# Cross attention on one core: four chunks' queries by seven products instead of eight, and the order written anew

## The chip, the cores and the metric

The kernel runs on one core of a Trainium2 chip. The metric is device time in microseconds (us), the median of three runs. All data are float32. The engines are TensorE (PE in the profile; its weight loads are PEld), VectorE (DVE), ScalarE (ACT), GpSimd (POOL) and SyncE (SP), which issues nearly all DMAs.

## What is computed

Two batches of 2048 tokens of 640 channels attend, with 20 heads of 32 channels, to a context of 154 tokens of 1024 channels. The first 77 context tokens (text) and the last 77 (image) have their own key and value weights and their own softmax; the two results are added.

```python
q = split_heads(x @ Wq.T)
k, v = split_heads(text @ Wk.T), split_heads(text @ Wv.T)
k_ip, v_ip = split_heads(ip @ Wk_ip.T), split_heads(ip @ Wv_ip.T)
out = merge(attend(q, k, v)) + merge(attend(q, k_ip, v_ip))   # softmax(q k / sqrt(32)) v
return out @ Wo.T + bo + x
```

The launch lays every matrix out with the contracted dimension first, so x is xT (640 x 4096), and the output is written as outT.

## The kernel before

Channels are cut into five chunks of 128 (four heads each), tokens into blocks of 512, four blocks in a batch. A *step* u is one chunk of one batch for two blocks (1024 tokens): twenty steps, q = u // 2 counts batch and chunk (0 to 4 are batch 0, 5 to 9 batch 1). A step's tokens are handled in three *groups* s: groups 0 and 1 of three tiles of 128 tokens ("large", 3 x 4 heads x 2 softmaxes of 77 = 1848 columns), group 2 of two tiles ("small", 1232 columns).

What is done for a step and group, each a word in a list:

- `q.u.h` (`queries`, L196, matmuls L201): the queries of one chunk for block h of step u, five matmuls of 512 columns over the five slices k of the contraction; `cq` scales them by ScalarE into a tile of `qpool` (L211).
- `Rs.u` (`scores`, L226): scores into four PSUM banks, one half of the eight (`@0` or `@1`).
- `Ks.u` (`take`, L245): ScalarE copies the four banks to SBUF (`pb`).
- `Ms.u` (`maxima`): VectorE's maximum of each row, from SBUF (L281), or, for the groups in `DIRECT`, from PSUM by four reductions (L284) with no K.
- `Ss.u` (`subtract`, L295): GpSimd subtracts the maxima. Groups in `DIRECT` and `BIASED` have no S: their exponential takes the maximum as its bias, row by row (L269), and those also in `SUMMED` get the row sums from it (no D).
- `Es.u` (exponential, L301 or L269, ScalarE), `Ds.u` (`sums`, L306, VectorE's denominators), `Is.u` (`invert`, L311, VectorE), `Ns.u` (`normalise`, L316, GpSimd), `Ts.u` (`transpose`, L323, VectorE).
- `A.q` (`attend`, L332): attention of both steps of a chunk; it waits for their six T. `CA` copies it out by ScalarE (L355, L359).

Around these stand the projections of keys and values (`k`, `v`, L142, with `ck`, `cv`), the output projection of batch 0 by seven products for eight (`m`, L490 and the fifth matmuls L500, taken by VectorE in `cm`, L515 and L521; GpSimd makes their token sums `G`, L431, and weight sums `W`, L401; `o` is the last chunk, L471), and, after A.9, the output projection of batch 1 by 33 products (`F`, L848) whose sums of weights and of rows (`V`, L828; `X`, L834) VectorE and GpSimd make, and whose results VectorE adds (`Y`, L792 and L794) and SP stores (L798).

The order is not derived at run time: `SCHEDULE` (L562) is a list of words, a planner's output, and `emit` issues them one after the other. Each engine executes its own words in the list's order, and waits only where data or a buffer demand it. SP's words are in the list too (`LK`, `LQ`, `LX` loads, `VS` spreads of values, `SF` and `SS` for batch 0's output), and one that waits holds the ones behind it.

Ahead of the list stands the opening (L524 to L559): loads of the first block by slices alternating with 64 KB slices of Wq on SP and ACT, the next loads, seven dummy matmuls (L549), queries of blocks 0 and 1 for chunk 0 and of block 0 for chunk 1, and the first two key projections.

Of the kernel before, what the change touches and what calls it, by code (L numbers as in the profile page):

```python
# [20 lines left out]
def kernel(  # L21
# [43 lines left out]
        (11, 0), (13, 0), (13, 2), (14, 0), (14, 2), (15, 1), (15, 2), (16, 2), (18, 1),  # L65
    }
    BIASED = {
        (2, 2), (3, 2), (4, 2), (5, 2), (6, 2), (7, 2), (9, 2), (11, 2), (12, 0), (12, 2), (18, 2), (19, 0),
        (19, 2),
    }  # L70
    SUMMED = {
        (4, 2), (6, 2), (11, 2), (12, 0), (12, 2), (13, 0), (13, 2), (14, 0), (15, 1), (15, 2), (18, 1),
        (18, 2), (19, 2),
# [7 lines left out]
    qpool = ctx.enter_context(tc.tile_pool(name="qpool", bufs=5))  # L81
    small = ctx.enter_context(tc.tile_pool(name="small", bufs=4))
    psum = ctx.enter_context(tc.tile_pool(name="psum", bufs=1, space=bass.MemoryType.PSUM))
# [3 lines left out]
    wqs = [const.tile([P, NC, P], F32, name=f"wq_{n}") for n in range(3)]  # L87
    bo_sb = const.tile([P, NC], F32, name="bo_sb")
    kT = const.tile([P, NC, B, 2, L], F32, name="kT")
# [77 lines left out]
    slices = []  # L167

    def load_x(queue=nc.sync):

        if slices:
            i, k = slices.pop(0)
            queue.dma_start(out=xs[i][:, k], in_=xT[ts(k, P), ts(i, TB)])

    XROOM = NHB - 1

    def place_of(u, h):
        _, b, _, sub = step_of(u)  # L180
        return late.index((u, h)) % XROOM if b else sub * NH + h

    def load_block(u, h):

        tokens = ds(S + (step_of(u)[3] * NH + h) * TB, TB)
        nc.sync.dma_start(
            out=xs[place_of(u, h)], in_=xT[:, tokens].rearrange("(k p) t -> p k t", p=P)
        )

    def load_wq(q):  # L190
        c = q % NC
        nc.sync.dma_start(
            out=wqs[q % 3], in_=WqT[:, ts(c, P)].rearrange("(k p) o -> p k o", p=P)
        )
# [3 lines left out]
    def queries(u, h, pq):  # L198
        q = step_of(u)[0]
        for k in range(NC):  # L200
# [7 lines left out]

    def take_queries(u, h, pq):
        qT = qpool.tile([P, TB], F32, tag="qT", name=f"qT_{u}_{h}")  # L210
        nc.scalar.mul(qT, pq, SCALE)  # L211
        qTs[(u, h)] = qT
# [13 lines left out]
    def scores(u, s, ps):  # L226
# [3 lines left out]
        for t in range(n):  # L230
            h, st = divmod(first + t, TB // P)
            for g in range(G):
# [6 lines left out]
                )  # L239

# [73 lines left out]
    def normalise(u, s):  # L314
        n = GROUPS[s][1] * G
        nc.gpsimd.tensor_tensor(  # L316
            rows_of(u, s), rows_of(u, s), rdens[(u, s)].unsqueeze(3).to_broadcast([P, n, 2, L]), ALU.mult
        )
# [205 lines left out]
    slices.extend((i, k) for i in range(NHB) for k in range(NC))  # L524
    queues = nc.sync, nc.scalar
    for k in range(NC):
        load_x(queues[k % 2])
        queues[1 - k % 2].dma_start(out=wqs[0][:, k, :], in_=WqT[ts(k, P), :P])
    for _ in range(NC):
        load_x()  # L530
    load_wq(1)
    half = NCC // 2
    for k in (0, half):
        nc.sync.dma_start(  # L534
            out=wo_ct[:, ds(k * B * LT, half * B * LT)].rearrange("p (k n) -> p k n", k=half),
            in_=ctxT[ds(k * P, half * P), :].rearrange("(k p) n -> p k n", p=P),
        )
        load_w(k // half)
    for _ in range(NH * NC):
        load_x()  # L540
    load_w(2)
    load_w(3)
    load_wq(2)
    nc.sync.dma_start(out=bo_sb, in_=bo.rearrange("(c p) -> p c", p=P))

    warm = pb[:, 0, 0].rearrange("p g l -> p (g l)")[:, :P]
    nc.vector.memset(warm, 0.0)
    for _ in range(7):
        nc.tensor.matmul(banks[0][:, :P], warm, warm, start=True, stop=True)  # L549
    FIRST = ((0, 0), (0, 1), (2, 0))  # L550
    for n, (u, h) in enumerate(FIRST):
        queries(u, h, banks[G + n])
        take_queries(u, h, banks[G + n])
    for t in range(2):

# [335 lines left out]
```

## Time and profile before

| | us |
|---|---|
| median of three runs | 497.44 |
| lowest and highest run | 497.38, 497.64 |
| span of the profiled execution | 496.7 |
| TensorE's first scores, start | 24.4 |
| attention of chunk 5, start | 254.7 |
| last matmul's add, start | 493.0 |

The span is the time from the first to the last instruction of the profiled execution, which is the only time the profile gives for it; the runs' median lies 0.7 us above. In the profile L12 is line 12 of the kernel. A row of a group of instructions reads: line, engine, operation, what it writes <- what it reads, shapes, count | busy us, mean ns of one | idle time of the engine before them, and what ended it. In the chain of waits the columns are start, length and what ran. In the table by stretches each engine's busy us stands before the number of its instructions in brackets.

### The profile page before, as it was taken

To read this page: it belongs to the slowest core of one execution; us is meant where nothing else is said; L and a number is where in the kernel's file an instruction comes from. 1 tells how busy PE (TensorE), PEld (TensorE's weight loads), DVE (VectorE), ACT (ScalarE), POOL (GpSimd) and SP (SyncE) were. 2 spreads that over 40 slices of the span, in tenths; PEclk is the share of its full clock that TensorE was granted. 3 is DMA by queue.
4 is the path that set the end of the run, shared out by engine and by line. 5 is a ranking of instruction groups with operands and counts; after the bars stand their busy time and mean duration, and the time that the engine had idled before them with its cause. 6 is when DMAs were issued, how large, how long until landed. Compare 5 with 4: busy or idle time off the path is not lost.

```text
span 496.7 us, 10482 instructions
## 1 busy us (share of the span) xinstructions
PE 490.3 (99%) x4114; PEld 287.9 (58%) x4114; DVE 408.5 (82%) x412; ACT 315.0 (63%) x1021; POOL 362.5 (73%) x157
## 2 busy tenths in 40 slices
PE   8999999999999999999999999999999999999997
PEld 5676657657547556456647654755755675444442
DVE  0069989979979989969976896687999978898877
ACT  1165878978978778668999786587578966100000
POOL 0069978798888999989874858565899888284830
PEclk9999999999999999999999999999999999999999
DMA  8991440332360454886445177418525401420115
GB/s 259 356 246 40 132 120 1 106 93 69 92 213 3 132 178 132 274 273 237 158 152 191 58 244 210 133 57 246 174 69 171 127 23 43 149 84 1 43 73 223
DMA packets 67474, 69.38 MB, mean 140 GB/s; under 512 B 5473, under 2 KB 47201, under 8 KB 67425
## 3 DMA queue, kind: packets, MB, share of 16 engines
q1 hardware_dynamic: 66704, 68.00, 43.8%
q8 instruction: 32, 0.52, 0.5%
q10 hardware_dynamic: 720, 0.72, 0.4%
q14 instruction: 18, 0.14, 0.1%
HBM read 54.94 MB, written 10.49 MB: 132 GB/s over the span
## 4 chain that ended last, share of the span: by engine, by line
PE 92%; DMA 3%; SPq 1%; DVE 1%; POOL 1%; ACT 1%; issue 0%; POOLq 0%
PE bank L201 33%; PE bank L848 11%; PE bank L490 10%; PE bank L233 10%; PE bank L332 10%; PE bank L142 9%; PE bank L471 6%; PE bank L500 3%; DMA aT<-in_L_xattn_Wk_ip_dram 2%; DMA wq<-in_L_xattn_Wq_dram 2%; SPq L534 1%; POOL pb L316 1%; DVE den L306 0%; ACT pb L301 0%; SPq L132 0%
## 5 line engine op out<-in xcount | busy, mean ns | idle before, releaser
L316 POOL TENSOR_TENSOR pb<-pb,rden 128x1848 f32<-128x1848 f32 (+1 forms) x60 | 176.1, 2944 | 39.7 <-DVE rden L311 35.5
L201 PE MATMUL bank<-x,wq 128*128 128x512 f32 x400 | 180.4, 601 | 0.6 <-DMA x<-in_x_dram 0.5
L295 POOL TENSOR_TENSOR pb<-pb,mx 128x1848 f32<-128x1848 f32 (+1 forms) x38 | 119.3, 3152 | 51.8 <-DVE mx L281 51.5
L201 PEld LDWEIGHTS bank<-x,wq 128*128 128x128 f32 x400 | 74.1, 191 | 86.7 <-issue 80.8
L323 DVE STREAM_TRANSPOSE pb<-pb 128x1920 f32<-128x1920 f32 (+1 forms) x60 | 115.7, 1932 | 4.9 <-POOL pb L316 4.3
L281 DVE TENSOR_REDUCE mx<-pb 128x24 f32<-128x1848 f32 (+1 forms) x51 | 93.7, 1850 | 30.7 <-ACT pb L245 30.5
L245 ACT COPY pb<-bank 128x462 f32<-128x462 f32 (+1 forms) x204 | 87.2, 539 | 36.0 <-PE bank L233 35.4
L306 DVE TENSOR_REDUCE den<-pb 128x24 f32<-128x1848 f32 (+1 forms) x47 | 88.7, 1895 | 17.6 <-ACT pb L301 13.3
L301 ACT ACTIVATE pb<-pb 128x1848 f32<-128x1848 f32 (+1 forms) x38 | 64.2, 1696 | 17.8 <-POOL pb L295 17.5
L269 ACT ACTIVATE pb<-pb,mx 128x77 f32<-128x77 f32 x224 | 67.8, 364 | 0.3 <-DVE mx L281 0.2
L233 PEld LDWEIGHTS bank<-kT,qT 32*128 32x128 f32 x1280 | 45.4, 184 | 26.9 <-issue 15.6
L269 ACT ACTIVATE pb<-bank,mx 128x77 f32<-128x77 f32 x184 | 51.8, 386 | 9.3 <-DVE mx L284 9.3
L233 PE MATMUL bank<-kT,qT 32*128 32x154 f32 x1280 | 56.2, 305 | 0.3 <-ACT kT L559 0.3
L332 PE MATMUL bank<-pb,v 32*32 32x512 f32 x1600 | 55.2, 597 | 0.0
L142 PE MATMUL bank<-wo_ct,aT 128*128 128x154 f32 x320 | 45.6, 296 | 0.3 <-DMA aT<-in_L_xattn_Wk_ip_dram 0.3
L142 PEld LDWEIGHTS bank<-wo_ct,aT 128*128 128x128 f32 x320 | 42.9, 188 | 3.6 <-issue 2.2
L332 PEld LDWEIGHTS bank<-pb,v 32*32 32x32 f32 x1600 | 29.9, 103 | 22.8 <-issue 10.7
L211 ACT ACTIVATE qT<-bank 128x512 f32<-128x512 f32 x40 | 24.2, 619 | 22.1 <-PE bank L201 22.0
L471 PE MATMUL bank<-aT,wo_ct 128*128 128x512 f32 x80 | 36.1, 596 | 0.0
L269 ACT ACTIVATION_READ_ACCUMULATOR pb<-bank,mx 128x1 f32 x128 | 33.6, 267 | 0.0
L490 PE MATMUL bank<-aT,wo_ct 128*128 128x256 f32 x128 | 32.3, 385 | 0.0
L490 PEld LDWEIGHTS bank<-aT,wo_ct 128*128 128x128 f32 x128 | 23.7, 190 | 6.5 <-issue 3.0
(75 smaller groups left out, 434.4 us busy)
## 6 DMA issues: line engine op xcount, KB each, us to landing
x<-in_x_dram SPq DMA_DIRECT2D x20, 1280.0 KB, 6.7
out_dram<-acc SPq DMA_DIRECT2D x20, 256.0 KB, 2.3
x<-in_x_dram SPq DMA_DIRECT2D x18, 256.0 KB, 5.9
acc<-in_x_dram SPq DMA_DIRECT2D x16, 256.0 KB, 4.7
out_dram<-x SPq DMA_DIRECT2D x15, 256.0 KB, 2.0
v<-vS SPq DMA_DIRECT2D x160, 20.0 KB, 2.8
wq<-in_L_xattn_Wq_dram SPq DMA_DIRECT2D x9, 320.0 KB, 5.0
aT<-in_L_xattn_Wk_dram SPq DMA_DIRECT2D x5, 512.0 KB, 5.5
```

The costliest lines, as they stand in the source:

```text
L142: nc.tensor.matmul(keys_in(out), loaded[n][:, k, :], cT[:, k, :, t, :], start=(k == 0), stop=(k == NCC - 1))
L201: nc.tensor.matmul(pq, wqs[q % 3][:, k, :], xs[place_of(u, h)][:, k, :], start=(k == 0), stop=(k == NC - 1),)
L233: nc.tensor.matmul(ps[g][:, ts(t, 2 * L)], qTs[(u, h)][g * D : (g + 1) * D, ts(st, P)], kT[g * D : (g + 1) * D, c, b].rearrange("p t l -> ...
L245: nc.scalar.copy(keys_of(u, s)[:, :, g], ps[g][:, : n * 2 * L].rearrange("p (n l) -> p n l", n=n))
L269: nc.scalar.activation(row, row if ps is None else rows_in(ps[g], n)[:, t, x], AF.Exp, bias=maxs[(u, s)][:, *one], accum_out=None if den i ...
L281: nc.vector.tensor_reduce(mx, rows_of(u, s), AX.X, ALU.max, negate=negate)
L295: nc.gpsimd.tensor_tensor(rows_of(u, s), rows_of(u, s), maxs[(u, s)].unsqueeze(3).to_broadcast([P, n, 2, L]), ALU.subtract)
L306: nc.vector.tensor_reduce(den_of(u, s), rows_of(u, s), AX.X, ALU.add)
L316: nc.gpsimd.tensor_tensor(rows_of(u, s), rows_of(u, s), rdens[(u, s)].unsqueeze(3).to_broadcast([P, n, 2, L]), ALU.mult)
L323: nc.vector.transpose(p, p)
L332: nc.tensor.matmul(pa[r][g * D : (g + 1) * D, :], v4s[q % 2][rows, g, k, :], zones[rows, :, g, k, :], start=(k == 0), stop=(k == NK - 1),)
L490: nc.tensor.matmul(part, w_of[m][:, kp, op], t_of(m, b, i)[:, kp], start=(op == kp == 0 and m in (1, 2, 5)), stop=(op == 1 and kp == 1 and ...
```

## The change

- **Queries of batch 1, chunks 0 to 3.** Chunks are taken in pairs (0, 1) and (2, 3). For a pair and a block, the four contraction slices form a 2 x 2 grid of two slices each, the block's tokens are halved (256 each), and the two chunks are the two outputs: a product of 2 x 2 blocks, made by seven products of sums instead of eight (`n`, `pair_product`, `take_pair`). The fifth slice is added into four of the products. Sums of tokens (`t`, four per block, GpSimd) and of weights (`WS`, GpSimd) are made once; the token sums of a block, 1 MB, are stored in DRAM (`TO`) and fetched again (`TI`) for the second pair. A product's result goes into PSUM; ScalarE writes four of the seven (`cn1`, `cn6`, `cn7`, `cn4`) to half a query tile, VectorE adds the other three.
- The query tiles so made early, for steps 12, 13, 16 and 17, are parked in DRAM (`QO`) and fetched again (`QI`). Chunk 4 of batch 1 and all of batch 0 keep the five matmuls.
- Blocks of batch 1 are loaded by `BX` (once for each pair) and, for chunk 4, `LX`.
- **Normalisations.** The nine groups in `SCALED` are normalised by VectorE.
- `DIRECT`, `BIASED`, `SUMMED` hold other groups.
- **Opening.** The first loads are words of the list (`XS`, `WA`, `LC`), fewer and larger, Wq's first two chunks together in rows of 1 KB; block 0 is multiplied by chunks 0 and 1 slice by slice (`qs`). Nine dummy matmuls.
- **End.** The last product `F32.0` and its add go by halves of 256 columns.
- **The list** is written anew; it holds 1172 words, before 1024.

What the two lists hold (the opening counted in; "to T" is up to the last transpose that chunk 5 needs):

| words | before | after |
|---|---|---|
| queries / products `n` / output products `m` in all | 40 / 0 / 28 | 24 / 56 / 28 |
| the same ahead of `A.5` | 29 / 0 / 4 | 20 / 37 / 6 |
| changes from scores or attention to other matmuls, in all (ahead of `A.5`) | 50 (27) | 51 (29) |
| groups in `DIRECT` / `BIASED` / `SUMMED` / `SCALED` | 9 / 13 / 13 / 0 | 17 / 10 / 13 / 9 |
| subtractions large / small, in all | 33 / 5 | 24 / 9 |
| normalisations on VectorE large / small, in all | 0 / 0 | 4 / 5 |
| to T: maxima from SBUF large / small | 24 / 13 | 19 / 9 |
| to T: maxima from PSUM large / small | 1 / 0 | 7 / 4 |
| to T: denominators large / small | 24 / 9 | 21 / 12 |
| to T: normalisations on VectorE large / small | 0 / 0 | 3 / 4 |
| to T: VectorE's products `cn`, `cm` | 0, 2 | 13, 3 |
| loads of a whole block | 20 | 12 |

The diff, cut to its core:

```diff
@@
     DIRECT = {
-        (11, 0), (13, 0), (13, 2), (14, 0), (14, 2), (15, 1), (15, 2), (16, 2), (18, 1),
+        (1, 1), (1, 2), (2, 0), (2, 2), (3, 1), (4, 1), (6, 1), (7, 1), (8, 1), (9, 2), (11, 2), (13, 0),
+        (13, 2), (15, 2), (16, 0), (19, 0), (19, 2),
     }
...
+    SCALED = {
+        (2, 2), (4, 0), (6, 2), (7, 2), (8, 0), (10, 0), (10, 2), (12, 1), (16, 2),
+    }
@@
+    FAR = [u for u in range(NC * SUB, NU - SUB) if (u // SUB - NC) % 2]
...
+    def put_away(u, h):
+        in_far[(u, h)] = far.tile([P, TB], F32, tag=f"qd_{u}_{h}", name=f"qd_{u}_{h}")
+        nc.sync.dma_start(out=in_far[(u, h)], in_=qTs.pop((u, h)))
+        q_free.append(q_place[(u, h)])
...
+    def sum_tokens(m, i, eng):
+        x, y = {
+            5: (tokens_in(i, 0, 0), tokens_in(i, 0, 1)),
+            7: (tokens_in(i, 0, 1), tokens_in(i, 1, 1)),
+            6: (sum_of(5, i), tokens_in(i, 1, 1)),
+            4: (sum_of(6, i), tokens_in(i, 1, 0)),
+        }[m]
+        eng.tensor_tensor(sum_of(m, i), x, y, ALU.add)
...
+    def pair_product(m, i, pair, ps):
+        w, last = weights_of(pair)
+        raw = {1: (0, 0), 2: (1, 0), 3: (1, 1)}
+        x = tokens_in(i, *raw[m]) if m in raw else sum_of(m, i)
+        fifth = {2: 0, 4: 0, 5: 1, 3: 1}.get(m)
+        for k in range(2):
+            nc.tensor.matmul(
+                ps[:, :HT],
+                w[m][:, k],
+                x[:, k],
+                start=(k == 0 and m in (1, 2, 5)),
+                stop=(k == 1 and fifth is None),
+                skip_group_check=True,
+            )
+        if fifth is not None:
+            nc.tensor.matmul(
+                ps[:, :HT],
+                last[m],
+                xs[i % 2][:, NC - 1, ts(fifth, HT)],
...
+    def take_pair(m, i, pair, ps):
+        u, h = 2 * (NC + 2 * pair) + i // NH, i % NH
+        if m in (7, 4, 5):
+            u += SUB
...
+        out = qTs[(u, h)][:, ts(int(m in (6, 3, 7, 5)), HT)]
+        if m in (1, 6, 7, 4):
+            nc.scalar.mul(out, ps[:, :HT], SCALE if m in (1, 4) else -SCALE)
+        else:
+            nc.vector.scalar_tensor_tensor(out, ps[:, :HT], SCALE, out, ALU.mult, ALU.add)
@@
-        nc.gpsimd.tensor_tensor(
+        (nc.vector if (u, s) in SCALED else nc.gpsimd).tensor_tensor(
             rows_of(u, s), rows_of(u, s), rdens[(u, s)].unsqueeze(3).to_broadcast([P, n, 2, L]), ALU.mult
         )
@@
-    for _ in range(7):
+    for _ in range(9):
         nc.tensor.matmul(banks[0][:, :P], warm, warm, start=True, stop=True)
...
+        "XS.0.0.1 WA.0.1 XS.0.1.1 WA.1.2 XS.0.3.1 XS.0.2.1 WA.3.2 XS.0.4.1 XS.1.2.3 XS.1.0.2 LC.0.4 LK.0 LC.4.4 LK.1 "
+        "LQ.2 qs.2.0.0.1@5 XS.2.0.2 XS.3.0.2 SF.0.3 XS.2.2.3 qs.0.0.0.1@3 qs.2.0.1.1 qs.0.0.1.1 qs.0.0.2.1 qs.0.0.3.1 "
+        "qs.0.0.4.1 XS.3.2.3 SF.0.2 SF.0.0 SF.0.1 SF.0.4 qs.2.0.2.1 qs.2.0.3.1 qs.2.0.4.1 cq.2.0 cq.0.0 LB "
+        "qs.0.1.0.1@2 qs.0.1.1.4 k.0.0@5 LK.4 cb.0.0.0 cb.0.0.1 k.0.1@0 cq.0.1 LK.3 LK.2 cb.0.1.0 cb.0.1.1 R2.0@1 "
+        "R0.0@0 K2.0 K0.0 M2.0 M0.0 S2.0 E2.0 LK.5 D2.0 S0.0 I2.0 N2.0 R1.0@1 K1.0 q.1.0@0 M1.0 E0.0 cq.1.0 S1.0 D0.0 "
...
+        "I1.7 E2.7 E0.7 D2.7 k.4.1@4 I2.7 q.8.1@7 D0.7 N2.7 T2.7 ck.4.1 k.4.0@0 ck.4.0 cq.8.1 BX.1 q.9.0@5 cq.9.0 "
+        "N1.7 R2.8@0 K2.8 M2.8 I0.7 t5.0.p WS.0.0 t6.0.p t7.0.p T1.7 R0.8@1 R1.8@0 t4.0.p K0.8 M0.8 N0.7 n1.0.0@4 "
+        "M1.8 T0.7 S0.8 v.4.1@7 TO.0 cn1.0.0 E2.8 D2.8 n6.0.0 cn6.0.0 E1.8 D1.8 E0.8 D0.8 I1.8 I2.8 q.9.1@5 n7.0.0 "
+        "cn7.0.0 n5.0.0@6 t5.1.p LQ.7 A.3@0 t7.1.p n4.0.0 I0.8 WS.0.1 CA.3 cv.4.1 cn5.0.0 t6.1.p N2.8 t4.1.p N0.8 "
...
+        "Y0.1.10 F32.0.0 F32.0.1 Y4.0.20.0 Y4.0.20.1 "
@@
+    def add_half(o, ps, op, half):
+        t, part = sum_at(o)[:, ts(half, HT)], ts(half, HT)
+        assert o not in untouched and parts_left[o] == 1
+        nc.vector.tensor_tensor(t, t, ps[:, part], op)
+        m, i = o
+        nc.sync.dma_start(out=outT[ts(m, P), ds(S + i * TB + half * HT, HT)], in_=t)
```

More of the change, by code (lines that the diff above doesn't have):

```diff
@@ L679, in emit @@
             queries(x, y, at[name])
+        elif k == "qs":
+            first, n = (int(a) for a in args[2:])
+            if where:
+                at[f"q.{x}.{y}"] = banks[int(where)]
+            queries(x, y, at[f"q.{x}.{y}"], range(first, first + n))
         elif k == "cq":
```

181 lines of the change are left out of this document (122 added, 59 removed), and 126 rows, old and new, of the table SCHEDULE.

## The prediction

> **What bounds the kernel now.** I read the page first, then the chain of waits in order of time, then who waits for whom, then busy time by stretches. The page names TensorE:
>
> ```profile
> span 496.7 us, 10482 instructions
> PE 490.3 (99%) x4114; PEld 287.9 (58%) x4114; DVE 408.5 (82%) x412; ACT 315.0 (63%) x1021; POOL 362.5 (73%) x157
> ```
>
> Busy matmuls need not be matmuls at their peak, so the chain has to say whether something else hides behind that 99%. Its columns are start, length, what; every TensorE matmul in float32 leaves two records, so "x10" is five matmuls.
>
> ```profile
> 13.68 8.00 DMA aT<-in_L_xattn_Wk_ip_dram
> ...
> 24.41 1.96 PE bank L233 x48
> 26.37 4.49 PE bank L201 x10
> ...
> 31.60 4.41 PE bank L142 x32
> 36.01 4.29 PE bank L201 x10
> ...
> 222.57 1.06 PE bank L490 x4
> 223.64 0.43 PE bank L500 x2
> 224.07 0.86 PE bank L490 x4
> ...
> 254.70 5.45 PE bank L332 x148
> ...
> 493.03 0.69 DVE acc L794
> ```
>
> Until 24.41 (the first scores) the chain waits for loads; from there to 493.03 it is matmul after matmul, and the end is one VectorE add and its store. The list of waits, asked for TensorE from 26 us to 496 us, has one entry in all:
>
> ```profile
> PE bank L490 <- DVE acc L515: 0.2, 1, 0.2
> ```
>
> So TensorE is the bound and its order runs without holes. An edit counts by what it does to TensorE's work, and by whether it opens a hole. The engine most likely to open one is VectorE, which makes the transposed probabilities that each attention word (L332) waits for:
>
> ```profile
> core 0: us, PE busy (x) PEld busy (x) DVE busy (x) ACT busy (x) POOL busy (x), PEclk, DMA share, GB/s
> 27.40:254.70 227.30, 227.13 (x2195) 137.99 (x2199) 209.34 (x163) 180.66 (x486) 198.22 (x71) 1.00 0.45 134
> 347.00:389.00 42.00, 42.00 (x392) 25.97 (x387) 39.86 (x38) 31.08 (x101) 38.34 (x16) 1.00 0.43 136
> ```
>
> From its first maximum (27.4) to the attention of chunk 5 (254.7) VectorE is idle for 227.3 - 209.3 = 18.0 us. That number is the whole question below.
>
> **The products (removed from TensorE).** A query word is five matmuls of 512 columns: 4.29 us in the row at 36.01. Four chunks by four blocks are sixteen such words, 68.6 us. In their place stand eight sets (two pairs of chunks by four blocks) of seven products. A product is two matmuls of 256 columns, and four of the seven carry a fifth: 18 matmuls, each 0.43 us by L490 (0.86 for two) and L500 (0.43 for one). That is 7.74 us a set, 61.9 us for eight: **6.8 us less** (6.7 to 6.9, with the rounding). Small matmuls could be held by their weight loads instead (the first row is the query line of today, for later):
>
> ```profile
> L201 PE MATMUL bank<-x,wq 128*128 128x512 f32 x400 | 180.4, 601 | 0.6 <-DMA x<-in_x_dram 0.5
> L490 PEld LDWEIGHTS bank<-aT,wo_ct 128*128 128x128 f32 x128 | 23.7, 190 | 6.5 <-issue 3.0 <-DVE acc L521 0.3 <-ACT pb L269 0.2
> ```
>
> A load takes 0.190 us and the matmul record beside it 0.215 (0.86 for four), so it fits, with little to spare; the new products have the shape of L490 and I price them by it. What is not hidden is the first load after scores or attention: 1.06 at 222.57, after scores, against 0.86 at 224.07, so 0.20. If each of the 56 products paid it the gain would be gone (11.2 us); but this falls due only where the kind of work changes. I count such changes in both lists: 50 and 51. I take +0.3 (0.2 for one more step out, about as much for the step in).
>
> **The opening.** The work before the first scores is the same: three queries and two key projections, 12.9 + 4.4 = 17.3 us (rows at 36.01 and 31.60), and so are the bytes ahead of the second key weights (two blocks, two chunks of Wq, the context, two key weights). What changes is the order: the first block is multiplied by two chunks as its slices land, so each slice gives twice the work, and the loads are fewer and larger. Nine dummy matmuls stand for seven:
>
> ```profile
> 1.05 3.35 PE L549 MATMUL bank<-pb 128*128 128x128 f32 x14 [1.05 <-DVE pb L547]
> ```
>
> They end at 1.05 + 9/7 x 3.35 = 5.4. If TensorE never starves after that, the scores begin at 5.4 + 17.3 + 0.3 (the copy of the keys) = 23.0; if the key weights land where they do now (13.68 + 8.00 = 21.7), at 24.4 again; and the second scores of the opening now need the half of PSUM that the first ones fill, so up to 0.5 of waiting for four copies is new. Bounds -1.4 and +0.5; I take **-0.4**.
>
> **The end.** The last matmul and its add go by halves, so that after the last matmul an add of 256 columns is left instead of 512: 0.69 becomes about 0.43 (L515 below); the store behind it stays. **-0.3** (0 to -0.5).
>
> **GpSimd.** Rows for both edits:
>
> ```profile
> L316 POOL TENSOR_TENSOR pb<-pb,rden 128x1848 f32<-128x1848 f32 x40 | 131.3, 3288 | 24.8 <-DVE rden L311 22.7 <-ACT aT L355 1.1 <-ACT pb L245 0.6
> L316 POOL TENSOR_TENSOR pb<-pb,rden 128x1232 f32<-128x1232 f32 x20 | 45.1, 2255 | 14.9 <-DVE rden L311 12.8 <-ACT kT L686 2.1
> L431 POOL TENSOR_TENSOR aT<-aT 128x512 f32<-128x512 f32 x8 | 10.2, 1278 | 0.1
> ```
>
> Four large and five small normalisations leave (24.4 us), nine large subtractions leave and four small ones come (about 20 us fewer at the price of L316); 16 token sums come at 1.28 (20.4) and eight weight sums of up to 256 columns (some 6). So 362 us becomes about 344: no bound by itself. But the sums stand close together, around chunks 3 to 5.
>
> **VectorE.** Rows for what changes ahead of chunk 5's attention:
>
> ```profile
> L281 DVE TENSOR_REDUCE mx<-pb 128x24 f32<-128x1848 f32 x35 | 71.5, 2051 | 28.4 <-ACT pb L245 28.3
> L281 DVE TENSOR_REDUCE mx<-pb 128x16 f32<-128x1232 f32 x16 | 22.6, 1409 | 2.3 <-ACT pb L245 2.2
> L284 DVE TENSOR_REDUCE mx<-bank 128x6 f32<-128x462 f32 x20 | 11.4, 631 | 5.7 <-ACT qT L211 3.0 <-PE bank L233 2.7
> L284 DVE TENSOR_REDUCE mx<-bank 128x4 f32<-128x308 f32 x16 | 6.5, 470 | 1.1 <-PE bank L233 1.1
> L515 DVE SCALAR_TENSOR_TENSOR acc<-bank,bo_sb,acc 128x256 f32<-128x256 f32 x32 | 13.7, 468 | 7.0 <-PE bank L500 7.0
> L834 DVE TENSOR_TENSOR pb<-aT 128x1024 f32<-128x1024 f32 x7 | 8.3, 1221 | 1.7 <-PE bank L332 1.5 <-ACT aT L359 0.2
> ```
>
> Up to the last transpose that chunk 5 needs (counts in the table of the change): five large maxima from SBUF fewer (-10.3), six more from PSUM at four reductions of 11.4/20 = 0.57 (+13.7); four small ones fewer (-5.6), four more from PSUM at 4 x 6.5/16 (+6.5); three large denominators fewer and three small ones more (same shapes as the maxima, -6.2 +4.2); 13 products taken at 13.7/32 = 0.43 (+5.6), one more output product (+0.9). Seven normalisations come. The trace shows none on VectorE: by a reduction of the same size one costs 2.05 and 1.41, by L834 scaled to its length 2.2 and 1.5. I take 2.1 and 1.4, so +11.9. Sum +20.7.
>
> In the same stretch TensorE gets more to do before chunk 5, because work moves ahead: 37 products (40.3) for nine queries (38.6), two output products (4.3), two more changes of kind (0.8): +6.8 less 0.4 of the opening. VectorE's first maximum comes about 1.2 earlier relative to the first scores (a small group is first). Idle time left: 18.0 + 6.4 + 1.2 - 20.7 = **4.9 us in 235**. It must work 98% of that stretch, where now it works 92%. After chunk 5 the room grows again, as fewer products are left.
>
> What made it idle so far:
>
> ```profile
> DVE mx L281 <- ACT pb L245: 29.4, 6, 26.4
> DVE den L306 <- ACT pb L301: 10.4, 10, 2.9
> ```
>
> (26.4 of the first row lies before the first maximum.) Most of the rest is denominators waiting for an exponential. An engine with more queued up waits less, and 17 groups instead of nine now go to ScalarE straight from PSUM without a subtraction, so I expect the 18 to shrink to 5 or 6, and give TensorE **+1.2** for what is left (0 to 4).
>
> [...] GpSimd and VectorE are seen to hold each other up, near the end:
>
> ```profile
> 421.10 0.46 POOL L828 TENSOR_TENSOR pb<-pb,wo_ct 128x128 f32<-128x128 f32 x1
> 436.31 1.22 DVE L834 TENSOR_TENSOR pb<-aT 128x1024 f32<-128x1024 f32 x1
> 436.48 1.37 POOL L828 TENSOR_TENSOR pb<-wo_ct,pb 128x128 f32<-128x128 f32 x1 [7.57 <-DVE pb L828]
> ```
>
> The same kind of GpSimd operation took 0.46 at 421.10 and 1.37 when it began 0.17 after a VectorE operation that reads two SBUF tensors; it ended 0.3 after that one did. [...] The normalisations moved to VectorE read two SBUF tensors. [...]
>
> **DMA and ScalarE**, at nothing. Twelve block loads stand for twenty (-10.5 MB); token sums and parked chunks go out and back (+12.6 MB).
>
> ```profile
> x<-in_x_dram SPq DMA_DIRECT2D x20, 1280.0 KB, 6.7
> out_dram<-acc SPq DMA_DIRECT2D x20, 256.0 KB, 2.3
> ```
>
> The new wait that matters: block 1's token sums, on GpSimd, overwrite block 0's, so they wait for a store of 1024 KB, at 2.3 to 6.7 us. Between them GpSimd has a normalisation and a subtraction, 2 x 3.29: covered, just. If not, two normalisations of step 8 are queued behind it, and chunk 4's attention waits for those. ScalarE, 63% busy, gets half-width copies and more rows of exponentials; it has the most room.
>
> **Sum.** -6.8 + 0.3 - 0.4 - 0.3 + 1.2 = -6.0: a span of 490.7. The profiled execution's span is 496.7, the median of the three runs 497.4, 0.7 more; so **491.4**. Without any waits it would be 490.2. A measurement of this kernel can tell about 0.2%, 1.0 us, from no change.
>
> **Rivals.**
> - *VectorE becomes the bound* (slower). Place: ahead of chunk 5. If its idle time stays at 18, chunk 5's attention is 18.0 - 4.9 = 13.1 late and nothing gives it back: 490.2 + 13.1 = 503.3. It decides from an idle time of 4.9 + 7.2 = 12.1 on. Were idle time the 5% of the stretch 347 to 389 (11.7 of 235), 6.8 late: 497.0, no gain. For it: 98% of 235 us, in an order with dependences. Against: in that stretch it ran at 95% and TensorE waited for nothing. Chance 0.14, of it 0.11 slower.
> - [...] Chance 0.08 (0.02 faster, 0.02 same, 0.04 slower).
> - *A store or fetch comes late.* One landing of 6.7 not covered: 496.9. Speaks for it: all such issues stand in one queue, SP's, behind waits of others; against: the load on them is hardly changed (+2 MB in all). Chance 0.04 (0.01, 0.02, 0.01).
> - That the products cost TensorE as much as the queries would need 0.48 a matmul instead of 0.43; L490 says no. Within the forecast's chance.
>
> **Chances.** The forecast's case 0.74 (489.2 to 495, waits of 0 to 5). Faster 0.77, same 0.07, slower 0.16. The range goes from 489.2 (an opening at its better bound) to 497.5, which takes in no gain; what is left out is nearly all VectorE as bound.
>
> **What would show it.** Right: the query line sums to some 108 us (24 of 40 words of 180.4) and the new product line to 62; attention of chunk 5 at about 261 + waits; VectorE over 95% busy up to there; TensorE's waits a few us in all. Wrong: product matmuls over 0.43; TensorE waiting for transposes (L323) or for copies before chunks 3 to 6; VectorE's normalisations well over 2.1 and 1.4, or GpSimd's over 3.3 beside them; first scores after 24.4.

## The result and the profile after

| | before | after |
|---|---|---|
| median of six runs each | 497.5 us | 517.7 us |
| lowest and highest | 497.4, 497.8 | 516.7, 521.5 |
| span of the profiled execution | 496.7 | 519.7 |
| first scores | 24.4 | 23.4 |
| attention of chunk 5 | 254.7 | 279.0 |
| last add | 493.0 | 515.9 |

The change makes the kernel 1.042 times as slow (95% interval 1.039 to 1.044), 20 us slower where 6 us faster were forecast. The execution that was profiled is the slowest of the six (521.5), so stretches of its trace can lie some 4 us above the median in sum. The page of after, its first rows and the granted clock in forty slices:

```profile
span 519.7 us, 11053 instructions
PE 495.9 (95%) x4248; PEld 320.8 (62%) x4248; DVE 445.3 (86%) x470; ACT 328.3 (63%) x1184; POOL 350.3 (67%) x169
...
PEclk9999999999999999979999999999999998999999
...
PE 58%; DVE 24%; ACT 11%; DMA 4%; issue 2%; SPq 0%; DVEq 0%; ACTq 0%
```

The clock row, all nines before, has a 7 and an 8. The last row is the chain of waits by engine. Before, TensorE held 92% of it; now VectorE, ScalarE and the DMAs hold 39%: TensorE's order has holes. It is still "busy" for 496 us, which shows how little that number says: matmuls at half clock count as busy (3.00 of 3.00 us in the second row by stretches below). The list of waits, asked for TensorE, its longest entries (us in total, times, longest):

```profile
PE bank L304 <- ACT qS L330: 8.2, 1, 8.2
PE bank L614 <- DVE acc L645: 3.9, 3, 2.5
PE bank L304 <- DMA x<-in_x_dram: 2.2, 1, 2.2
PE bank L353 <- ACT kT L818: 1.4, 1, 1.4
```

Before, the same list had one entry of 0.2 us behind the opening. The largest stop, in the chain in order of time (start, length, what):

```profile
211.88 0.68 PE bank L304 x4
212.56 6.66 DMA x<-in_x_dram
219.22 0.02 issue
219.24 0.51 SPq L164
...
219.85 0.53 SPq L293
...
220.48 4.28 DMA qd<-qS
...
224.87 0.39 ACT qS L330
...
225.40 2.05 PE bank L304 x4
```

Read from below: product `n4.2.0` (L304 at 225.40) adds into the bank of `n7.2.0`, which ScalarE must first write into a query tile (`cn7.2.0`, L330). A tile is free only when the queries parked in it have been stored in DRAM (`QO.12.1`, the DMA qd<-qS, issued at 220.48). SP issued it so late because `BX.3` (a block of 1280 KB), the eight spreads of `VS.4.1` (L164) and `TO.2` (L293) stand ahead of it in the list: the last spread went out at 219.24, when the block had landed. The queries to be stored were ready some 7 us earlier: ScalarE's last copy into them (`cn4.1.0`, 0.58 us at 212.67) ended at 213.25. In e2, below, the same store goes out at 212.4.

What this stop does to the clock, by stretches (the columns are those of the table in the prediction):

```profile
217.10:225.40 8.30, 0.06 (x5) 0.03 (x1) 4.84 (x4) 0.53 (x2) 7.08 (x5) 0.77 0.63 231
225.40:228.40 3.00, 3.00 (x7) 2.47 (x8) 1.85 (x2) 1.19 (x5) 0.33 (x1) 0.50 0.15 33
228.50:231.00 2.50, 2.50 (x13) 2.22 (x12) 1.81 (x2) 2.50 (x15) 2.50 (x2) 1.00 0.35 105
```

TensorE stands still for 8.2 us, then runs 3.0 us at a granted clock of 0.50, then at 1.00 again. The 0.77 of the first row says that the half clock was granted before the stop was over: by the clock's record in the trace from 221.6 to 228.4. The four product records at 225.40 took 2.05 where 0.86 was priced.

VectorE, by stretches:

```profile
26.50:279.00 252.50, 240.30 (x2290) 164.29 (x2288) 234.50 (x218) 194.22 (x658) 198.91 (x89) 0.99 0.47 143
100.00:200.00 100.00, 97.22 (x1069) 64.11 (x1067) 98.88 (x78) 75.03 (x229) 75.60 (x34) 1.00 0.39 115
200.00:279.00 79.00, 69.58 (x596) 53.99 (x590) 67.52 (x72) 59.30 (x224) 69.09 (x38) 0.96 0.67 216
```

From 100 to 200 us it is busy for 98.9 of 100; up to the attention of chunk 5 (279.0) for 93%, where over 95% was named as a sign. And the groups that the forecast named as signs: the large normalisations left on GpSimd, the queries, and the nine on VectorE (last two rows):

```profile
L440 POOL TENSOR_TENSOR pb<-pb,rden 128x1848 f32<-128x1848 f32 x36 | 118.2, 3288 | 44.0 <-DVE rden L435 32.2 <-ACT pb L369 7.4 <-ACT aT L479 3.8
L217 PE MATMUL bank<-x,wq_pair 128*128 128x512 f32 x200 | 89.5, 599 | 0.0
...
L217 PE MATMUL bank<-x,wq 128*128 128x512 f32 x40 | 18.0, 597 | 0.0
...
L440 DVE TENSOR_TENSOR pb<-pb,rden 128x1848 f32<-128x1848 f32 x4 | 15.7, 3935 | 0.0
...
L440 DVE TENSOR_TENSOR pb<-pb,rden 128x1232 f32<-128x1232 f32 x5 | 11.2, 2241 | 0.1
```

The queries make 107.5 us, as forecast; the products, summed from each record's start to the next one's, 69.8 where 62 was named. A large normalisation takes VectorE 3.9 us, a small one 2.2, where 2.1 and 1.4 were taken: 26.9 us for the nine. How that comes about, in VectorE's timeline (first row) and GpSimd's (second; one of its operations ends at 109.87, this is the next):

```profile
109.94 5.12 DVE L440 TENSOR_TENSOR pb<-pb,rden 128x1848 f32<-128x1848 f32 x1
```

```profile
109.83 3.29 POOL L440 TENSOR_TENSOR pb<-pb,rden 128x1848 f32<-128x1848 f32 x1
```

GpSimd's large normalisation began 0.11 us before VectorE's and ends at 113.1, after 3.29 us, the mean of all 36 (3.288); VectorE's ends at 115.1, 1.94 us behind it, and three of e4's four large ones (below) average 2.08. So it seems to have done nothing from 109.9 to 113.1. The prediction read the like off one GpSimd operation near the end (1.37 us for 0.46, at 436.48); now VectorE is the one that waits. What follows calls this the lock.

### The profile page after: what moved, and what is told of

Its sections match the earlier page's. It is cut to its first block, busy times and chain, and to the rows that moved or that the text cites. A ratio compares the mean times of both kernels' runs of the same rounds, so it can differ in the third digit from the quotient of the medians.

```text
span 519.7 us, 11053 instructions
## 1 busy us (share of the span) xinstructions
PE 495.9 (95%) x4248; PEld 320.8 (62%) x4248; DVE 445.3 (86%) x470; ACT 328.3 (63%) x1184; POOL 350.3 (67%) x169
## 4 chain that ended last, share of the span: by engine, by line
PE 58%; DVE 24%; ACT 11%; DMA 4%; issue 2%; SPq 0%; DVEq 0%; ACTq 0%
PE bank L217 11%; PE bank L990 11%; ACT pb L393 9%; PE bank L304 7%; PE bank L614 6%; PE bank L353 6%; DVE pb L447 5%; DVE den L430 5%; PE bank L148 5%; PE bank L595 4%; PE bank L456 4%; DVE mx L405 4%; DVE pb L440 3%; DMA x<-in_x_dram 3%; DVE mx L408 2%
## 5 line engine op out<-in xcount | busy, mean ns | idle before, releaser
L440 POOL TENSOR_TENSOR pb<-pb,rden 128x1848 f32<-128x1848 f32 (+1 forms) x51 | 151.7, 2984 | 59.3 <-DVE rden L435 47.5
L419 POOL TENSOR_TENSOR pb<-pb,mx 128x1848 f32<-128x1848 f32 (+1 forms) x33 | 99.0, 3005 | 63.2 <-DVE mx L405 63.0
L405 DVE TENSOR_REDUCE mx<-pb 128x24 f32<-128x1848 f32 (+1 forms) x43 | 79.6, 1857 | 35.7 <-ACT pb L369 35.5
L393 ACT ACTIVATE pb<-bank,mx 128x77 f32<-128x77 f32 x352 | 92.2, 392 | 10.8 <-DVE mx L408 10.7
L217 PE MATMUL bank<-x,wq_pair 128*128 128x512 f32 x200 | 89.5, 599 | 0.0
L369 ACT COPY pb<-bank 128x462 f32<-128x462 f32 (+1 forms) x172 | 74.2, 535 | 14.6 <-PE bank L353 14.1
L353 PEld LDWEIGHTS bank<-kT,qT 32*128 32x128 f32 x1280 | 49.9, 186 | 23.6 <-issue 13.3
L217 PEld LDWEIGHTS bank<-x,wq_pair 128*128 128x128 f32 x200 | 37.5, 192 | 43.2 <-issue 42.8
L425 ACT ACTIVATE pb<-pb 128x1848 f32<-128x1848 f32 (+1 forms) x33 | 54.5, 1669 | 12.8 <-POOL pb L419 12.8
L393 ACT ACTIVATION_READ_ACCUMULATOR pb<-bank,mx 128x1 f32 x168 | 43.7, 264 | 0.0
L408 DVE TENSOR_REDUCE mx<-bank 128x6 f32<-128x462 f32 (+1 forms) x68 | 33.8, 558 | 2.8 <-PE bank L353 2.8
```

What stands on the lines that cost most here:

```text
L217: nc.tensor.matmul(pq, wqs[q % 3][:, k, :], xs[place_of(u, h)][:, k, :], start=(k == 0), stop=(k == NC - 1),)
L353: nc.tensor.matmul(ps[g][:, ts(t, 2 * L)], qTs[(u, h)][g * D : (g + 1) * D, ts(st, P)], kT[g * D : (g + 1) * D, c, b].rearrange("p t l -> ...
L369: nc.scalar.copy(keys_of(u, s)[:, :, g], ps[g][:, : n * 2 * L].rearrange("p (n l) -> p n l", n=n))
L393: nc.scalar.activation(row, row if ps is None else rows_in(ps[g], n)[:, t, x], AF.Exp, bias=maxs[(u, s)][:, *one], accum_out=None if den i ...
L405: nc.vector.tensor_reduce(mx, rows_of(u, s), AX.X, ALU.max, negate=negate)
L419: nc.gpsimd.tensor_tensor(rows_of(u, s), rows_of(u, s), maxs[(u, s)].unsqueeze(3).to_broadcast([P, n, 2, L]), ALU.subtract)
```

## The experiments

Fifteen kernels, in five questions. Ratios are to the kernel before, whose median was 497.5 to 497.8 on each chip used. "Attention of chunk k" is the start of the first matmul of `A.k`.

### Is it the normalisations on VectorE?

**e1: all nine back on GpSimd.**

```diff
-    SCALED = {(2, 2), (4, 0), (6, 2), (7, 2), (8, 0), (10, 0), (10, 2), (12, 1), (16, 2)}
+    SCALED = set()
```

> The kernel after, with all sixty normalisations on GpSimd. In the kernel after, the nine on VectorE take 26.9 us of it, some 11 of them waiting for GpSimd. Theory L (VectorE with the lock is what holds the kernel): VectorE has 27 us more room, the holes of TensorE before chunk 3 (some 5 us) and at 423 to 432 (4 us) go; 503 to 510. Theory S (the store that comes late, behind other transfers in SP's queue, holds it): the 8 us hole at 217 stays and the rest hardly matters; 514 to 518.

Measured: 521.5 us, ratio 1.048 (1.046 to 1.049), slower than the change as it is and outside both theories' ranges. Attention of chunk 2 comes earlier (141.7 for 143.9), that of chunk 4 later (234.2 for 231.8): in its trace GpSimd works without a pause from 167 to 226 us, and TensorE still stops for 7.8 us at 220.

**e4: the kernel before, with the nine on VectorE.** The set `SCALED` and the line that uses it are all that is added.

> The kernel before, with the same nine normalisations on VectorE and nothing else changed. Theory L: they take 2.5 to 3 us each with the lock, 23 in all, in place of the 2 on GpSimd that its chain could spare; VectorE's 18 us of idle time before chunk 5 are used up; 500 to 507. Theory S: nothing is stored late here; 497 to 499.

Measured: 504.9, ratio 1.014 (1.012 to 1.016): 7.1 us for the nine alone. In this list GpSimd holds them up little; the rows of L319, their line there:

```profile
L319 DVE TENSOR_TENSOR pb<-pb,rden 128x1848 f32<-128x1848 f32 x4 | 9.4, 2344 | 0.1
L319 DVE TENSOR_TENSOR pb<-pb,rden 128x1232 f32<-128x1232 f32 x5 | 7.1, 1429 | 0.1
```

16.5 us for the nine, not 26.9 (one large one took 3.13, so the other three average 2.08). So what costs 7 us here is hardly the lock.

**e12: as e4, a reduction in place of each of the nine.** A second sum over the same rows takes VectorE 2.08 us for a large group and 1.42 for a small one, about as long as most normalisations in e4 (2.08 and 1.43), and has one input.

```diff
+        if (u, s) in SCALED:
+            return nc.vector.tensor_reduce(dens[(u, s)], rows_of(u, s), AX.X, ALU.add)
         nc.gpsimd.tensor_tensor(
```

> The kernel before with a second sum over the rows on VectorE in place of the nine normalisations (those rows stay unnormalised): the same occupation of VectorE, no second input, GpSimd relieved of nine. Beside e4 (the nine normalisations on VectorE in the list of before, 504.9), where the nine took 16.5 us together, almost their time alone. Theory O' (in this list it is VectorE's occupation, some 15 us, that costs the 7 us, not the lock): 503 to 505. Rival L (the lock costs it here too): 497.5 to 500.

Measured: 503.9, ratio 1.013 (1.011 to 1.014). Of e4's 7.1 us the lock has about 1.0; the rest comes with 15 us more work for VectorE, though VectorE had 18 us of idle time in this list. About half of it is lost between the attention of chunks 2 and 4 (70.9 us for 67.6), around three of the nine. That the idle time lies elsewhere is a guess.

The next four have the store of e2 (below; 510.7) in them, so that the stop at 217 us does not cover what they tell.

**e5: the nine left out altogether** (those rows stay unnormalised).

```diff
+        if (u, s) in SCALED:
+            return
```

> The kernel of e2 (the store ahead, 510.7) with the nine normalisations of VectorE left out altogether: their probabilities stay unnormalised. Theory V: the nine cost VectorE some 27 us in the trace of the changed kernel (nine instructions of 1.4 to 5.1 us), VectorE has no room ahead of chunk 5, so that time comes back where VectorE sets the end: 494 to 501, with attention of chunk 5 near 262 (270.8 in e2). Rival W: what holds e2 back is the list's order, copies behind maxima and sums on VectorE and ScalarE, whatever the nine cost: 505 to 511.

Measured: 502.9, ratio 1.011 (1.009 to 1.012). 7.8 us come back, fewer than expected, and attention of chunk 5 comes at 266.6 (270.8 in e2), not 262. Even without the nine's work the kernel is slower than before: something else costs more than the products save.

**e6: a reduction in place of each of the nine,** the edit of e12 in the list of after.

> The kernel of e2 with each of the nine normalisations replaced on VectorE by a second sum over the same rows (a reduction, 1.35 or 2.0 us in the trace, one input and a small output, so the same time as a normalisation beside an idle GpSimd); these rows stay unnormalised. It takes away only what the normalisation and GpSimd do to each other. Theory L (the lock is the larger half: 11 of the nine's 27 us, and GpSimd's own operations beside them are stretched as well): 501 to 506. Rival O (VectorE's occupation alone counts): within 1.5 us of e2's 510.7.

Measured: 503.6 in the median (503.4 to 509.2, four runs; ratio 1.016, 1.010 to 1.022, wide for one run of 509.2). The reductions' rows:

```profile
L441 DVE TENSOR_REDUCE den<-pb 128x24 f32<-128x1848 f32 x4 | 8.3, 2069 | 0.0
L441 DVE TENSOR_REDUCE den<-pb 128x16 f32<-128x1232 f32 x5 | 7.1, 1420 | 0.1
```

15.4 us of VectorE's time, and the kernel is 0.7 us slower than with nothing in their place. So in the list of after it is the other way round than in that of before: occupation costs 0.7 us, what the normalisation and GpSimd do to each other 7.1. Theory L holds, and its share is larger than it expected.

**e7: five of the nine back on GpSimd.**

```diff
-    SCALED = {(2, 2), (4, 0), (6, 2), (7, 2), (8, 0), (10, 0), (10, 2), (12, 1), (16, 2)}
+    SCALED = {(7, 2), (8, 0), (10, 0), (10, 2)}
```

> The kernel of e2 with five of the nine back on GpSimd, those at which GpSimd has idle time in the trace (2.2, 4.0, 6.2, 12.1, 16.2 by chunk and group); 7.2, 8.0, 10.0 and 10.2, beside the token sums, stay on VectorE. Theory V: some 15 us of VectorE's time come back, GpSimd's idle time takes the five: 503 to 508. Rival P: GpSimd has no room either, as with all nine on it (521.5): 511 or more.

Measured: 509.5, ratio 1.023 (1.022 to 1.025), 1.2 us for the five. Both theories missed: what VectorE gains, GpSimd's queue seems to take; that is not shown.

**e9: the nine on GpSimd, the products' sums left out** (`t` all, `WS` but for the fifth chunk's).

```diff
+        elif k[0] == "t":
+            pass
```

> The kernel of e2 with the nine normalisations back on GpSimd and with the token sums (16 a half, line 287) and the weight sums (all but the fifth chunk's) of the queries' products left out, so that the products work on wrong inputs. Theory G (GpSimd has no room for the nine because the sums, some 30 us of it between 169 and 250 us, stand there; that is why moving the nine back alone gave 521.5 and 519.8): 498 to 505, like the run without the nine (502.9). Rival: the nine on GpSimd hold the list up whatever else stands there, since the list is planned for them on VectorE: 510 or more.

Measured: 508.7, ratio 1.022 (1.020 to 1.023). Between the two: against e3 (the nine on GpSimd with the sums, 519.8) the sums have 11 us, but the nine on GpSimd still cost 6 us more than left out (e5, with the sums in). A likely reason, not shown: the groups stand in the list where VectorE, not GpSimd, has its turn.

### Is it the late store?

**e2: `QO.12.1` ahead of the block and the spreads,** right behind the copy that it waits for.

```diff
-        ... n3.1.0 BX.3 M0.10 VS.4.1 cn3.1.0 cn4.1.0 T0.9 TO.2 T1.9 n6.2.0 QO.12.1 N2.9 ...
+        ... n3.1.0 M0.10 cn3.1.0 cn4.1.0 QO.12.1 BX.3 VS.4.1 T0.9 TO.2 T1.9 n6.2.0 N2.9 ...
```

> The kernel after, with one store (QO.12.1) directly behind its last product and ahead of the block load and the value spread that stood before it. Theory S: the store lands some 8 us earlier, the 8.2 us hole at 217 and the half clock after it go: 507 to 510. Theory L: VectorE and ScalarE are late anyway and take the time back within a chunk or two: 514 to 517.

Measured: 510.7, ratio 1.025 (1.023 to 1.028). SP's timeline there:

```profile
212.38 0.34 SPq L240 DMA_DIRECT2D qd<-qS  x1
212.82 0.39 SPq L202 DMA_DIRECT2D x<-in_x_dram  x1
213.26 6.90 SPq L164 DMA_DIRECT2D v<-vS  x8
```

The store goes out at 212.4 for 220.5, the stop at 217 is gone (0.7 and 1.2 us stay nearby), no half clock follows, and attention of chunk 4 comes at 222.1 for 231.8. 7.1 us for the place of one word; theory S, with 507 to 510, was nearly right.

**e3: both, the store ahead and the nine on GpSimd.**

> Both edits. If the two causes are separate parts of the loss, the gains add: by L and S together 495 to 502. If one hides the other, it is no better than the better of the two.

Measured: 519.8, ratio 1.043 (1.041 to 1.046). The stop at 217 is gone and another of 7.2 us stands at 237.7, with 10.2 us at half clock from 240.1 on; this one waits for a VectorE copy. That copy stands behind a transpose, and for this VectorE had waited for a normalisation on GpSimd (list of waits, VectorE, 228 to 250 us):

```profile
DVE pb L445 <- POOL pb L438: 8.1, 1, 8.1
```

So the gain of e2 and the move of e1 do not add: GpSimd, which in e1 works 58.6 of the 59 us from 167 to 226, then sets when things come.

### What stops TensorE at 423 and 430 us?

In after, products of the output projection wait there for VectorE's adds out of PSUM (L645, 3.9 us in the list of waits).

**e8: three of these adds ahead of a transpose and a sum** (on e2).

```diff
-        ... V.X.0.p T0.18 G6.3 cm1.3 SS.3.0 ...   p.1@4 D1.19 cm3.3 cm6.3 m7.3 ...
+        ... V.X.0.p cm1.3 T0.18 G6.3 SS.3.0 ...   p.1@4 cm6.3 cm3.3 D1.19 m7.3 ...
```

> The kernel of e2 with three of VectorE's copies out of product banks at the end (after attention of chunk 8) ahead of a transpose and a sum that stand before them in the list. Theory E: TensorE's two stops at 411.1 and 417.6 (1.1 and 2.5 us) go, and with them the 3.4 us at half clock right behind: 505.5 to 508. Rival: the next wait takes it, 509.5 to 511.

Measured: 511.0, ratio 1.027 (1.023 to 1.030), no gain: three stops of 0.9 to 1.3 us stand at 417 to 424 instead, with 6.8 us at half clock. What was put back is, it seems, needed there too.

**e11: three weight sums behind these adds instead** (on e2). `V.H`, `V.T` and `V.O` go behind `cm6.3`.

> The kernel of e2 with three of VectorE's weight sums for the last outputs (V.H, V.T, V.O, of 0.95 to 2.3 us there) moved from between the copies out of the product banks to behind the last of these copies but one. Theory E': these sums are what the copies queue behind; the stops at 411.1 and 417.6 shrink from 3.7 to under 1.5 us and the half-clock window behind them goes: 506 to 508.5. Rival: the copies wait for the reductions and transposes there, as when these were moved (511.0): 510 to 511.5.

Measured: 507.2, ratio 1.021 (1.018 to 1.023): 3.5 us. Of the stops of 1.1 and 2.5 us there one of 1.0 is left, and the half clock behind them is gone. VectorE's timeline of after, between the adds:

```profile
419.71 0.94 DVE L969 TENSOR_TENSOR pb<-wo_ct,pb 128x128 f32<-128x128 f32 x1
...
424.02 0.95 DVE L969 TENSOR_TENSOR pb<-pb,wo_ct 128x128 f32<-128x128 f32 x1
...
427.08 1.47 DVE L969 TENSOR_TENSOR pb<-wo_ct 128x128 f32<-128x128 f32 x1
```

and of e11, behind them:

```profile
417.86 0.29 DVE L970 TENSOR_TENSOR pb<-wo_ct,pb 128x128 f32<-128x128 f32 x1
418.06 0.28 DVE L970 TENSOR_TENSOR pb<-pb,wo_ct 128x128 f32<-128x128 f32 x1
418.26 0.28 DVE L970 TENSOR_TENSOR pb<-wo_ct 128x128 f32<-128x128 f32 x1
```

The same three operations take 3.4 us there and 0.85 here: they too have two SBUF inputs, and at the first place each ends 0.15 us behind a GpSimd operation (those end at 420.50, 424.82 and 428.40); such an operation took 0.28 in before at 436.11, with GpSimd idle.

### What is the opening worth?

**e10: the kernel before with the new opening alone.** Loads, the pair of weights, the order of the first queries and the nine dummies as after; from the first scores on the list of before.

> The kernel before with the new opening alone (the loads in the new order and pieces, the pair of weights in one tile, queries of (2,0) and (0,0) interleaved, nine warming matmuls); from the first scores on its list is the one of before. By the prediction's term 0.4 us less (bounds 1.4 less to 0.5 more), by the 1.0 us that the first scores come earlier in the changed kernel's trace: 496.5 to 497.3. Rival: the first wait behind it takes it back: no difference from before.

Measured: 501.0, ratio 1.006 (1.005 to 1.007): 3 us slower, neither case. TensorE's waits there, and the clock (span of the stretch first):

```profile
PE bank L143 <- DMA aT<-in_L_xattn_Wv_dram: 2.3, 1, 2.3
```

```profile
33.10:36.50 3.40, 3.40 (x15) 3.40 (x14) 2.38 (x2) 2.25 (x2) 3.40 (x2) 0.50 0.01 2
```

The scores do start at 23.0, but the first value projection, which the list of before has earlier than that of after, finds its weights (`LK.2`) still under way: 2.3 us, and 3.4 at half clock.

**e13: the same with `LK.2 LK.3` ahead of the last block of tokens.**

```diff
-        "... XS.2.0.2 XS.3.0.2 XS.2.2.3 ... LK.3 LK.2 ..."
+        "... XS.2.0.2 XS.2.2.3 LK.2 LK.3 XS.3.0.2 ..."
```

> The opening alone (e10, 501.0) with the loads of the third and fourth key and value weights issued ahead of the last blocks of tokens, as in the list of before. In e10's trace the first scores start at 23.0 (24.4 before), but TensorE stops 2.3 us at 30 us for these weights and runs 3.4 us at half clock behind. Theory F (that stop and its half clock are all that e10 loses, so 4.0 us of it go): 496 to 497. Rival: the tokens' blocks, later by 1 MB, stop TensorE instead: 498 or more.

Measured: 497.0 against 497.5, ratio 0.9987 (0.9978 to 0.9996), eleven runs: 0.5 us (0.2 to 1.1) faster than before, the only one of all kernels here that is. TensorE's timeline at that place has no stop:

```profile
22.97 1.85 PE L246 MATMUL bank<-kT,qT 32*128 32x154 f32 x48 [0.31 <-ACT kT L650]
...
29.98 4.48 PE L143 MATMUL bank<-wo_ct,aT 128*128 128x154 f32 x32
34.30 4.45 PE L211 MATMUL bank<-x,wq_pair 128*128 128x512 f32 x10
```

Attention comes about 1.5 us earlier for every chunk (chunk 9: 422.1 for 423.6), and the profiled span is 495.2 for 496.7; the medians lie only 0.5 apart. The difference lies in the profile of before. In all runs of these experiments the time is 1.7 to 1.9 us above the span of the same execution, so a span of 496.7 goes with a time of about 498.5, 1 us above the median of before (the 0.7 set above between span and median compares two executions). And e4 and e12, which have the old opening, start their first scores at 23.3, not at 24.4: in the profile of before the second key weights landed at 21.68, in that of e12 at 20.54. The opening is worth the 0.5 of the medians.

### Do the shares add up, and what is left?

**e14: store ahead, weight sums later, reductions for the nine.**

> The changed kernel with three things undone at once: the store ahead (e2), the three weight sums later (e11), a sum in place of each of the nine normalisations (e6; those rows stay unnormalised). If the shares add up (7.1, 3.5 and 7.1 us of 517.7): 499 to 501. Rival: they overlap, the time saved at one place being waited for at the next: 502 or more.

Measured: 501.2, ratio 1.006 (1.004 to 1.008). Apart the three were worth 7.1, 3.5 and 7.1, together they are worth 16.5 of these 17.7: nearly additive.

**e15: as e14, the nine and the products' sums left out.**

> As the last kernel, but with the nine normalisations left out altogether and the token sums and weight sums of the queries' products left out too: no work that the change adds to VectorE and GpSimd is left but the copies out of the products. Theory R (what is still lacking to the forecast is room on these two engines): 490 to 495. Rival W (it is the list's order and the copies behind ScalarE): 497 to 500.

Measured: 501.5 (499.3 to 505.3), ratio 1.008 (1.005 to 1.011): not faster than e14. From 100 to 200 us (the columns as before):

```profile
100.00:200.00 100.00, 99.38 (x1087) 67.44 (x1086) 89.52 (x81) 75.83 (x227) 64.83 (x24) 1.00 0.43 127
```

VectorE has room again (89.5 of 100) and GpSimd too (64.8), and it does not help. Theory R fell, and its rival's 497 to 500 is passed as well. What is left shows in TensorE's own order. Summed from each matmul record's start to the next one's, queries and products take 171.5 us in e15 and 178.2 before, 6.7 less. But 1.8 of this lies ahead of the first scores (13.0 for 14.8), in the new opening and the late loads of before: behind them they take 158.5 for 163.4, 4.9 less. And the 1280 records of scores take 60.0 for 53.6. Measured from a score word's first record to its last, none of the 60 words before takes over 0.25 us more than the fastest of its size; in e15 ten do, the worst 1.6, and the excess is 13.2 us in sum for 6.1. A likely reason is that the scores are issued before their PSUM banks have been read out; the list of waits names such a reader for one stop of 1.0 us (ScalarE's exponentials, L394), for the rest it is not shown. Which readers to move for that was not tried.

## Why the prediction was wrong, step by step

- **Products: nearly right, 4.9 us for 6.5.** The sum had 6.8 less and 0.3 for changes of kind; the traces of e15 and before give 4.9 behind the opening. Both sides of the difference were low: from start to start the products take 66.7 for 61.9, and the queries removed had 71.6 for 68.6. The term for changes of kind was too small: 0.3 where 1.9 came out. In the products' excess some 0.5 is a wait (L305 in e15's list); the greater part is about 0.1 at each passage to and from other work (in after the four product records at 314.80, behind scores, take 0.97 to the next one's start, for 0.86).
- **Opening: right in size, in part by luck.** Alone it is worth 0.5 for the 0.4 taken, if two weight loads are moved ahead (e13); without that, in the list of before, it costs 3 (e10). But the bounds were counted from 24.4, in a profile whose weights had landed late: the first scores start at 23.4 in after and between 22.4 and 23.6 in all traces with the new opening, and at 23.3 with the old one in e4 and e12. In the list of after the second scores start too early: the bound said up to 0.5 for them. The chain of after shows the three first score words together:

```profile
23.36 3.30 PE bank L353 x64
```

  Before, 48 records took 1.96, so 64 should take 2.6; 0.7 is waiting.
- **DMA "at nothing": wrong, 7.1 us.** This step hides the longest stop. The prediction looked at one new wait, of GpSimd for a store of token sums, and found it covered. It did not follow the other new stores through SP's queue: `QO.12.1` frees a tile of `qpool` that a product needs, and stands behind 1280 KB and eight spreads. The rival *a store or fetch comes late* names the place in so many words (one queue, behind waits of others) but got a chance of 0.04, "the load on them is hardly changed". Load was not the point, order was. And a late landing was priced at 6.7, without what a stop does to the clock.
- **What GpSimd and VectorE do to each other: wrong, 7.1 us.** The row at 436.48 had shown one GpSimd operation held up beside VectorE (1.37 us for 0.46); the sum has no term of its own for this, and a loss by it got a chance of 0.08. All nine normalisations but one run beside a GpSimd operation in after, at 26.9 us instead of the 15.4 of equal reductions (2.07 and 1.42 each in e6): 9.0 more were measured for the seven ahead of chunk 5, 11.5 for all nine, and what of it reached the end is 7.1.
- **VectorE's room, 4.9 us in 235: the count was near, the conclusion was not.** In e6, without the lock, VectorE is busy 227.2 us from its first maximum to the attention of chunk 5, and the sum said 209.3 + 20.7 = 230.0. But its idle time there is 13.7 us, and in after 18.0, as much as before: that the 18 would "shrink to 5 or 6" was hoped. With the lock the seven normalisations take 9.0 more, so the room was below nothing, and VectorE was busy 98.9 of 100 us from 100 to 200. *VectorE becomes the bound* (503.3) is what e4 and e12 show in part, in the list of before. But e5 and e15 show that giving VectorE its room back does not bring the forecast.
- **The end, "-0.3": wrong, 3.5 us or more.** The prediction looked at the last matmul alone, and not even there did the 0.3 come: both half adds follow the last matmul, 0.75 us for the 0.69 of one add, and from its end to the end of the span it is 3.9 us for 3.7.

```profile
515.85 0.75 DVE L925 TENSOR_TENSOR acc<-acc,bank 128x256 f32<-128x256 f32 x2 [0.42 <-PE bank L990]
```

  The list's end was written anew as well, with three weight sums between the adds that TensorE waits for.
- **Waits, +1.2 (0 to 4): wrong.** Besides the three above (16.5 us together), e14 is 9.8 us over the forecast; its trace shows 6.4 of this in the scores (60.0 us, as in e15) and 2.2 in the products, and why the scores wait stays open. Behind the opening no step of the prediction asked when a score word's banks come free; it took it that nothing would wait, as in the list of before. That list was closer to its limits than "matmul after matmul" says: from 301.3 to 312.4 us its chain runs through an exponential, a sum, a normalisation, a transpose and two adds (the normalisation 3.30 us at 306.10).

Three causes of 3 to 7 us each, undone one by one and together, and a fourth of 6 that is only read off the traces, stood where the sum had next to nothing; any two of them take the gain of 6.

## What to carry to other kernels

A planned list without holes is one particular list: when it is planned anew, the price of the edited operations is the smaller part, and every new wait must be followed, word by word, to the queue it stands in (what is ahead of it on SP, and who waits for the buffer that it frees). Before moving work from GpSimd to VectorE, count how many of the moved operations will stand beside a GpSimd operation, and price these at their own time plus what is left of the other's (5.12 us at 109.94: 3.2 left of GpSimd's, then 1.9). A bound engine's gain of 1% can be lost by one word's place: here one store put ahead of a block load and eight spreads is worth more than all that the new products save (7.1 us for 4.9).

## What the runs showed of the hardware

- **A stop of TensorE cost more than its length.** Late in it or shortly after it the granted clock fell to 0.50: by the clock's record for 6.827 us from 4.4 us into the stop of 8.24 in after, for 3.413 behind each of the stops of 2.2 and 2.5 there (from 310.3 and from 433.2), and for 10.240 from 2.4 us into that of 7.2 in e3. Of the twelve stops of 2.2 to 2.6 us in these traces ten had such a window, two had none (e1 at 430.8, e5 at 412.3); stops under 1.8 us standing alone had none, but the three of e8 together had 6.8 us. Why two had none is not shown.
- **The lock showed both ways:** in after VectorE's large normalisation took 5.12 us at 109.94, beside one GpSimd operation of 3.29, where three in e4 average 2.08; a sum of 128x128 on VectorE took 1.47 at 427.08, beside a GpSimd operation, and 0.28 in before at 436.11, with GpSimd idle. A reduction over a large group kept its 2.02 us at 107.55, beside a GpSimd normalisation (107.61 to 109.87). The other way round, in after:

```profile
190.77 3.98 DVE L440 TENSOR_TENSOR pb<-pb,rden 128x1848 f32<-128x1848 f32 x1
192.77 3.12 POOL L287 TENSOR_TENSOR x<-x,x 128x512 f32<-128x512 f32 x1
```

  VectorE's normalisation stands beside one on GpSimd that ends at 192.81 and itself ends 1.94 us behind it, at 194.75; the token sum that GpSimd begins meanwhile takes 3.12 us for its usual 1.28 and ends 1.1 behind it. So in this kernel an engine waits not only where data or a buffer demand it.
- **SP's issues waited for an earlier landing:** in after the last of eight spreads went out (219.24) only when the block load issued eight before it had landed (219.22), and in e2 it was the same (issued at 219.65, the block landed at 219.63). So in this kernel a large load ahead of small ones held all that stood behind them, 6.7 us here.
